# Gate products of a GRU graph network as 2x2 block products with seven multiplications

## The chip, the cores and the metric

The kernel runs on one core of a Trainium2 chip. The metric is the device time of one execution in microseconds (us). The profile is one execution recorded by the hardware profiler. Its engines are PE (TensorE matmuls), PEld (TensorE weight loads, which run beside PE), DVE (VectorE), ACT (ScalarE), POOL (GpSimd) and SP (SyncE, which here only issues transfers).

## The reference

There are 128 graphs of 128 nodes with 256 features, all float32. Layer 0 is a gated graph network of three steps, and layer 1 is a graph attention layer:

```python
A = (adj != 0)
h = relu(layernorm(x))
for i in range(3):
    m = einsum('bnd,de->bne', h, weight[i])
    aggr = einsum('bst,bsd->btd', A, m)
    gi = aggr @ w_ih.T + b_ih ; gh = h @ w_hh.T + b_hh      # 3 gates of 256 each
    r = sigmoid(i_r + h_r) ; z = sigmoid(i_z + h_z)
    n = tanh(i_n + r * h_n)
    h = (1 - z) * n + z * h
x = x + h

h = relu(layernorm(x)); Wh = h @ W; s = Wh.sum(-1)
e = leaky_relu(s[:, :, None] + s[:, None, :], 0.2), -inf where adj == 0
x = x + softmax(e) @ Wh
```

## The kernel before, in words

A group is four graphs (`G`), so 512 nodes (`GN`); there are 32 groups. Features lie on partitions in two chunks of 128 (`KD`) whenever a gate product reads them: `hT` (the state) and `aT` (the aggregate of the state over the graph) are tiles of 128 x 2 x 512. In the setup the kernel transposes `w_hh` into `w_hhT`, and multiplies each layer's message weight with `w_ih` into `w_x`, so that the gates read the aggregate directly.

A GRU step (one layer of one group) is `aggregate` (L191, one 128x128 matmul for each graph and chunk) and two calls of `gru_half`, one for each output chunk `j`. A half forms four sums in PSUM with `gate_sum` (L203): the reset gate r from state and aggregate, the state part and the aggregate part of the candidate n, and the update gate z. Each sum is built of matmuls of 128x128 weights with 512 columns; a half has 12 of them, a step 24. ScalarE evaluates r (L212), n (L219) and z (L222); VectorE forms u (L215, L217) and the new state `new` (L224 to L226). Between layers `T_to_rows` (L181) transposes the state back to node rows, which ScalarE copies (L250), because the aggregation needs them as the stationary operand. VectorE copies the aggregate out of PSUM (L193).

Around the three steps a group has a layer norm with transposes (`normed`, `rows_to_T`, L159), and after them the residual and the second layer norm (L254, L149), the product with `W` (L170), the attention scores (L268 to L282), the transposes of the weights `e` (L286), their product with `Wh` (L294) and the output (L297, L300).

`group` is a generator that yields between these pieces. Two streams of groups (even and odd) are advanced in turns, one seven pieces ahead of the other (`LAG`), so that one stream's other work stands between the GRU steps of the other:

```python
LAG = 7
streams = [stream(0), stream(1)]
for _ in range(LAG):
    next(streams[0])
while streams:
    for s in list(streams):
        if next(s, s) is s:
            streams.remove(s)
```

The three steps of a group follow each other on TensorE, and then come the three steps of the other stream's group. The order within each engine's queue is fixed when the program is built, by a scheduler that takes the program's order as priority and moves ready work forward; the engines then wait for each other through semaphores. PSUM has eight banks of 512 float32 columns: five for the gates (`ps_gate`) and three for everything else (`ps_misc`).

Of the kernel before, what the change touches and what calls it, by code (L numbers as in the profile page):

```python
# [8 lines left out]
F32 = mybir.dt.float32  # L9
I32 = mybir.dt.int32  # L10
AF = mybir.ActivationFunctionType
OP = mybir.AluOpType
AX = mybir.AxisListType

P = 128
G = 4
EPS = 1e-5
ALPHA = 0.2
BIG = 3.0e38
# [3 lines left out]
def kernel(  # L23
# [19 lines left out]
    nc = tc.nc  # L43
    B, N, D = x.shape
    L = weight.shape[0]
    KD = D // P
    NG = B // G
    GN = G * N
    assert N == P and D == 2 * P and B % G == 0

    const = ctx.enter_context(tc.tile_pool(name="const", bufs=1))
    loads = ctx.enter_context(tc.tile_pool(name="loads", bufs=4))
    small = ctx.enter_context(tc.tile_pool(name="small", bufs=4))
    setup_ctx = ExitStack()
    setup = setup_ctx.enter_context(tc.tile_pool(name="setup", bufs=1))
    ps_gate = ctx.enter_context(tc.tile_pool(name="ps_gate", bufs=5, space=bass.MemoryType.PSUM))
    ps_misc = ctx.enter_context(tc.tile_pool(name="ps_misc", bufs=3, space=bass.MemoryType.PSUM))

    loaded = {}

    def load(g):
        if g >= NG:
            return
        xt = loads.tile([P, G, D], F32, name="xt")
        nc.sync.dma_start(xt, x[g * G:(g + 1) * G].rearrange("b n d -> n b d"))
        at = loads.tile([P, G, N], I32, name="at")
        nc.sync.dma_start(at, adj[g * G:(g + 1) * G].rearrange("b n m -> n b m"))
        loaded[g] = xt, at

# [27 lines left out]

    w_t = []
    for name, nat in zip(("w_hhT", "w_ihT"), w_nat):
        t = (const if name == "w_hhT" else setup).tile([P, KD, 3 * D], F32, name=name)  # L100
        for k in range(KD):
            for c0 in range(0, 3 * KD, 3):
                ps = ps_misc.tile([P, 512], F32, name="misc")
                for c in range(3):
                    nc.tensor.transpose(ps[:, c * P:(c + 1) * P],
                                        nat[:, c0 + c, k * P:(k + 1) * P], ident)
                nc.vector.tensor_copy(t[:, k, c0 * P:(c0 + 3) * P], ps[:, :3 * P])
        w_t.append(t)
# [6 lines left out]
    for layer in range(L):  # L115
        wT = setup.tile([P, KD, D], F32, name="w_msgT", bufs=L)
        for e in range(KD):
            ps = ps_misc.tile([P, 512], F32, name="misc")
            for k in range(KD):
                nc.tensor.transpose(ps[:, k * P:(k + 1) * P],  # L120
                                    w_msg[:, layer, k, e * P:(e + 1) * P], ident)
            nc.scalar.copy(wT[:, e, :], ps[:, :D])
        t = const.tile([P, KD, 3 * D], F32, name="w_x", bufs=L)
        for k in range(KD):
            for g0, gn in ((0, 512), (512, 3 * D - 512)):
                ps = ps_misc.tile([P, 512], F32, name="misc")
                for e in range(KD):
                    nc.tensor.matmul(ps[:, :gn], wT[:, e, k * P:(k + 1) * P],  # L128
                                     w_ihT[:, e, g0:g0 + gn], start=(e == 0), stop=(e == KD - 1))
                nc.vector.tensor_copy(t[:, k, g0:g0 + gn], ps[:, :gn])  # L130
        w_x.append(t)

    setup_ctx.close()
    work = ctx.enter_context(tc.tile_pool(name="work", bufs=3))


    def normed(src, name):
        st = small.tile([P, G, 6], F32, name="bn_st")
        mv = small.tile([P, G, 2], F32, name="bn_mv")
        for b in range(G):  # L140
            nc.vector.bn_stats(st[:, b, :], src[:, b, :])  # L141
        for b in range(G):
            nc.vector.bn_aggr(mv[:, b, :], st[:, b, :])
        rs = small.tile([P, G], F32, name="rstd")
        nc.gpsimd.tensor_tensor(rs, mv[:, :, 1], eps, OP.add)
        nc.gpsimd.tensor_tensor(rs, rs, neghalf, OP.pow)  # L146
        y = work.tile([P, G, D], F32, name=name)
        for b in range(G):
            nc.vector.tensor_scalar(y[:, b, :], src[:, b, :], mv[:, b, 0:1], rs[:, b:b + 1],  # L149
                                    op0=OP.subtract, op1=OP.mult)  # L150
        return y
# [33 lines left out]
    def aggregate(m, a):  # L185

        aT = work.tile([P, KD, GN], F32, name="aT")
        for k in range(KD):
            ps = ps_misc.tile([P, 512], F32, name="misc")
            for b in range(G):  # L190
                nc.tensor.matmul(ps[:, b * N:(b + 1) * N], m[:, b, k * P:(k + 1) * P], a[:, b, :],  # L191
                                 start=True, stop=True)
            nc.vector.tensor_copy(aT[:, k, :], ps[:, :GN])  # L193
        return aT

    def gate_sum(c, terms):

        ps = ps_gate.tile([P, GN], F32, name="gate")
        n = len(terms) * KD
        for i in range(n):  # L200
            w, t = terms[i // KD]
            k = i % KD
            nc.tensor.matmul(ps, w[:, k, c * P:(c + 1) * P], t[:, k, :],  # L203
                             start=(i == 0), stop=(i == n - 1))
        return ps

    def gru_half(j, w_ihT, hT, aT, new):

        cr, cz, cn = j, KD + j, 2 * KD + j
        p_r = gate_sum(cr, [(w_hhT, hT), (w_ihT, aT)])  # L210
        r = work.tile([P, GN], F32, name="r")
        nc.scalar.activation(r, p_r, AF.Sigmoid, bias=bias_s[:, cr:cr + 1])  # L212
        p_hn = gate_sum(cn, [(w_hhT, hT)])
        u = work.tile([P, GN], F32, name="u")
        nc.vector.scalar_tensor_tensor(u, p_hn, bias_h[:, cn:cn + 1], r, op0=OP.add, op1=OP.mult)  # L215
        p_in = gate_sum(cn, [(w_ihT, aT)])
        nc.vector.tensor_tensor(u, u, p_in, OP.add)  # L217
        n = work.tile([P, GN], F32, name="n")
        nc.scalar.activation(n, u, AF.Tanh, bias=bias_i[:, cn:cn + 1])  # L219
        p_z = gate_sum(cz, [(w_hhT, hT), (w_ihT, aT)])  # L220
        z = work.tile([P, GN], F32, name="z")
        nc.scalar.activation(z, p_z, AF.Sigmoid, bias=bias_s[:, cz:cz + 1])  # L222
        d = work.tile([P, GN], F32, name="d")
        nc.vector.tensor_tensor(d, hT[:, j, :], n, OP.subtract)  # L224
        nc.vector.tensor_tensor(d, d, z, OP.mult)  # L225
        nc.vector.tensor_tensor(new[:, j, :], n, d, OP.add)  # L226

    def group(g):

        xt, at = loaded.pop(g)  # L230
        load(g + 2)
        a = work.tile([P, G, N], F32, name="a")
        nc.vector.tensor_scalar(a, at, 0.0, None, op0=OP.not_equal)
        y = normed(xt, "h")
        rows = work.tile([P, G, D], F32, name="rows")
        nc.scalar.activation(rows, y, AF.Relu)
        yield
        hT = rows_to_T(rows, "hT", 4)
        yield
        for layer in range(L):  # L240
            aT = aggregate(rows, a)
            new = work.tile([P, KD, GN], F32, name="hT", bufs=4)
            gru_half(0, w_x[layer], hT, aT, new)
            yield
            gru_half(1, w_x[layer], hT, aT, new)
            hT = new
            yield
            if layer < L - 1:
                rows = work.tile([P, G, D], F32, name="rows")
                T_to_rows(hT, lambda b0, ps: nc.scalar.copy(rows[:, b0:b0 + 2, :], ps))  # L250
                yield

        x1 = work.tile([P, G, D], F32, name="x1")
        T_to_rows(hT, lambda b0, ps: nc.vector.tensor_tensor(  # L254
            x1[:, b0:b0 + 2, :], xt[:, b0:b0 + 2, :], ps, OP.add))
        h = normed(x1, "h")
        yield
        h1T = rows_to_T(h, "h1T", 2, AF.Relu)
        yield
        wh = rows_product(h1T, w1, "wh")  # L260
        s = small.tile([P, G], F32, name="s")
# [5 lines left out]
        for b in range(G):  # L267
            nc.tensor.transpose(p_s[:, b, :], s[:, b:b + 1].to_broadcast([P, P]), ident)  # L268
        e = work.tile([P, G, N], F32, name="e")
        nc.vector.tensor_scalar(e, at, 0.0, -BIG, op0=OP.is_equal, op1=OP.mult)  # L270
        nc.vector.tensor_tensor(e, e, p_s, OP.add)
        nc.vector.tensor_tensor(e, e, s[:, :, None].to_broadcast([P, G, N]), OP.add)
        nc.vector.scalar_tensor_tensor(e, e, ALPHA, e, op0=OP.mult, op1=OP.max)
# [13 lines left out]
        eT = work.tile([P, G, N], F32, name="eT")  # L287
        nc.scalar.copy(eT, p_e)
        yield
        o = work.tile([P, G, D], F32, name="o")  # L290
        for b0 in range(0, G, 2):
            ps = ps_misc.tile([P, 2, D], F32, name="misc")
            for b in range(2):
                nc.tensor.matmul(ps[:, b, :], eT[:, b0 + b, :], wh[:, b0 + b, :],  # L294
                                 start=True, stop=True)
            for b in range(2):
                nc.vector.scalar_tensor_tensor(o[:, b0 + b, :], ps[:, b, :],  # L297
                                               rden[:, b0 + b:b0 + b + 1], x1[:, b0 + b, :],
                                               op0=OP.mult, op1=OP.add)
        nc.gpsimd.dma_start(out[g * G:(g + 1) * G].rearrange("b n d -> n b d"), o)  # L300
        yield


# [41 lines left out]
```

## Time and profile before

| | |
|---|---|
| median of 3 runs | 2614.0 us (2613.59 to 2614.19) |
| profiled execution | 2614.36 us, span 2612.6 us, TensorE clock granted 0.994 |
| PE | 2547.0 us busy, 97% of the span |
| PEld | 1357.0 us, 52% |
| DVE | 1282.0 us, 49% |
| ACT | 720.8 us, 28% |
| POOL | 104.1 us, 4% |
| HBM | 27.79 MB read, 16.78 MB written, 17 GB/s over the span |

The span runs from the first to the last instruction. A line of the groups names the program line, engine and operation, what is written and read, the shape and the count, then the busy time and mean duration of one, then the engine's idle time before it and what ended that. Each float32 matmul stands in the trace as two records. Matmuls are pipelined and their ends are modelled, so the distance from start to start tells what one costs in a row of them. In a timeline the columns are the start, the duration and then the group, with the idle time before it and its releaser in brackets.

### The profile page before, as it was taken

Reading aid. Unit: us, or ns where it says so; the run is one execution under the profiler, and the core shown is the slowest. Engines: PE = TensorE matmul, PEld = TensorE weight load, DVE = VectorE, ACT = ScalarE, POOL = GpSimd, SP = SyncE. Lnnn points to the kernel's source line nnn. Section 1 sums busy time; section 2 is a strip of 40 time slices with the busy share of each in tenths; the row PEclk is TensorE's granted clock in tenths of the full one; section 3 lists DMA queues with packets and bytes.
Section 4 is the critical chain, followed back from the end, with each engine's and each line's share of the span. In section 5 each row is a group of like instructions: output and inputs, shape, how many; then the busy total and the mean of one; then the engine's idle time right before and its main releaser. Section 6 shows DMA issues by size and latency. Waiting matters only on the chain.

```text
span 2612.6 us, 22325 instructions
## 1 busy us (share of the span) xinstructions
PE 2547.0 (97%) x8532; PEld 1357.0 (52%) x8532; DVE 1282.0 (49%) x2487; ACT 720.8 (28%) x1063; POOL 104.1 (4%) x166
## 2 busy tenths in 40 slices
PE   6999999999999999999999999999999999999996
PEld 4455555555555555555555555555555555555553
DVE  3355454555545455454554545555454554545544
ACT  1223222332222322222232223322223222222322
POOL 0000000000000000000000000000000000000000
PEclk9999999999999999999999999999999999999998
DMA  3000000000000000000000000000000000000000
GB/s 101 1 21 21 9 21 20 15 18 12 17 21 21 13 21 13 16 21 13 20 21 9 21 21 15 19 13 17 21 21 12 21 9 16 17 9 8 9 1 17
DMA packets 42700, 46.01 MB, mean 18 GB/s; under 512 B 3168, under 2 KB 38496, under 8 KB 42592
## 3 DMA queue, kind: packets, MB, share of 16 engines
q1 hardware_dynamic: 33792, 25.17, 3.2%
q0 software_dynamic: 4608, 16.78, 1.8%
q10 hardware_dynamic: 4192, 2.63, 0.4%
q8 instruction: 67, 1.10, 0.2%
q14 instruction: 41, 0.34, 0.0%
HBM read 27.79 MB, written 16.78 MB: 17 GB/s over the span
## 4 chain that ended last, share of the span: by engine, by line
PE 87%; DVE 6%; issue 2%; ACT 2%; POOL 1%; DMA 1%; ACTq 0%; POOLq 0%; DVEq 0%
PE gate L203 69%; PE misc L191 7%; PE misc L170 4%; PE misc L181 3%; PE misc L294 2%; DVE h L149 1%; DVE bn_st L141 1%; POOL rstd L146 1%; PE misc L159 1%; ACT z L222 1%; DVE hT L226 1%; DVE d L225 1%; ACT L222 1%; PE misc L268 1%; PE misc L128 0%
## 5 line engine op out<-in xcount | busy, mean ns | idle before, releaser
L203 PE MATMUL gate<-hT,w_hhT 128*128 128x512 f32 x2304 | 1096.5, 593 | 0.0
L203 PE MATMUL gate<-aT,w_x 128*128 128x512 f32 x2304 | 1093.5, 596 | 0.0
L203 PEld LDWEIGHTS gate<-aT,w_x 128*128 128x128 f32 x2304 | 427.4, 190 | 553.7 <-issue 477.5
L203 PEld LDWEIGHTS gate<-hT,w_hhT 128*128 128x128 f32 x2304 | 419.2, 191 | 431.3 <-issue 407.2
L215 DVE SCALAR_TENSOR_TENSOR u<-gate,bias_h,r 128x512 f32<-128x512 f32 x192 | 144.0, 750 | 417.7 <-PE gate L203 417.7
L212 ACT ACTIVATE r<-gate,bias_s 128x512 f32<-128x512 f32 x192 | 132.1, 688 | 726.0 <-PE gate L203 726.0
L219 ACT ACTIVATE n<-u,bias_i 128x512 f32<-128x512 f32 x192 | 138.8, 723 | 610.8 <-DVE u L217 540.8
L225 DVE TENSOR_TENSOR d<-d,z 128x512 f32<-128x512 f32 x192 | 132.6, 691 | 238.1 <-ACT z L222 236.5
L222 ACT ACTIVATE z<-gate,bias_s 128x512 f32<-128x512 f32 x192 | 131.8, 687 | 272.4 <-PE gate L203 271.0
L191 PEld LDWEIGHTS misc<-a,rows 128*128 128x128 f32 x1536 | 185.4, 193 | 17.4 <-issue 11.6
L224 DVE TENSOR_TENSOR d<-hT,n 128x512 f32<-128x512 f32 x192 | 131.9, 687 | 124.0 <-ACT n L219 123.9
L191 PE MATMUL misc<-a,rows 128*128 128x128 f32 x1536 | 188.4, 276 | 0.0
L217 DVE TENSOR_TENSOR u<-u,gate 128x512 f32<-128x512 f32 x192 | 131.3, 684 | 116.2 <-PE gate L203 115.8
L193 DVE COPY aT<-misc 128x512 f32<-128x512 f32 x192 | 130.0, 684 | 40.0 <-PE misc L191 39.7
L181 PE MATMUL misc<-ident,hT 128*128 128x128 f32 x768 | 119.9, 278 | 22.1 <-DVE hT L226 16.9
L226 DVE TENSOR_TENSOR hT<-n,d 128x512 f32<-128x512 f32 x192 | 132.3, 689 | 4.4
L181 PEld LDWEIGHTS misc<-ident,hT 128*128 128x128 f32 x768 | 87.6, 141 | 75.4 <-DVE hT L226 48.3
L170 PE MATMUL misc<-w,h1T 128*128 128x256 f32 x512 | 121.6, 386 | 0.6 <-ACT h1T L160 0.5
L170 PEld LDWEIGHTS misc<-w,h1T 128*128 128x128 f32 x512 | 95.7, 192 | 24.8 <-issue 7.2
L250 ACT COPY rows<-misc 128x512 f32<-128x512 f32 x128 | 69.1, 591 | 100.7 <-PE misc L181 100.7
L262 DVE TENSOR_REDUCE s<-wh 128x4 f32<-128x1024 f32 x32 | 39.0, 1220 | 109.3 <-ACT wh L172 109.3
L300 POOL DMA_DIRECT2D out_dram<-o x32 | 25.6, 802 | 1296.7 <-DVE o L297 1259.5
(60 smaller groups left out, 1201.1 us busy)
## 6 DMA issues: line engine op xcount, KB each, us to landing
xt<-in_x_dram SPq DMA_DIRECT2D x32, 512.0 KB, 3.9
out_dram<-o POOLq DMA_DIRECT2D x32, 512.0 KB, 3.4
at<-in_adj_dram SPq DMA_DIRECT2D x32, 256.0 KB, 2.8
w_msg<-in_L_gnn_weight_dram ACTq DMA_DIRECT2D x1, 768.0 KB, 7.0
w_hh_nat<-in_L_gnn_w_hh_dram ACTq DMA_DIRECT2D x1, 768.0 KB, 10.6
w_ih_nat<-in_L_gnn_w_ih_dram ACTq DMA_DIRECT2D x1, 768.0 KB, 13.8
w<-in_L_gnn_W_dram ACTq DMA_DIRECT2D x1, 256.0 KB, 9.0
bias_i<-in_L_gnn_b_ih_dram ACTq DMA_DIRECT2D x1, 3.0 KB, 11.8
```

What stands on the lines that cost most here:

```text
L170: nc.tensor.matmul(ps[:, b, :], srcT[:, k, (b0 + b) * N:(b0 + b + 1) * N], w[:, k, :], start=(k == 0), stop=(k == KD - 1))
L181: nc.tensor.transpose(ps[:, b, k * P:(k + 1) * P], srcT[:, k, (b0 + b) * N:(b0 + b + 1) * N], ident)
L191: nc.tensor.matmul(ps[:, b * N:(b + 1) * N], m[:, b, k * P:(k + 1) * P], a[:, b, :], start=True, stop=True)
L203: nc.tensor.matmul(ps, w[:, k, c * P:(c + 1) * P], t[:, k, :], start=(i == 0), stop=(i == n - 1))
L212: nc.scalar.activation(r, p_r, AF.Sigmoid, bias=bias_s[:, cr:cr + 1])
L215: nc.vector.scalar_tensor_tensor(u, p_hn, bias_h[:, cn:cn + 1], r, op0=OP.add, op1=OP.mult)
L217: nc.vector.tensor_tensor(u, u, p_in, OP.add)
L219: nc.scalar.activation(n, u, AF.Tanh, bias=bias_i[:, cn:cn + 1])
L222: nc.scalar.activation(z, p_z, AF.Sigmoid, bias=bias_s[:, cz:cz + 1])
L224: nc.vector.tensor_tensor(d, hT[:, j, :], n, OP.subtract)
L225: nc.vector.tensor_tensor(d, d, z, OP.mult)
L226: nc.vector.tensor_tensor(new[:, j, :], n, d, OP.add)
```

## The change

The columns of a step's nodes are split into two halves of 256 (`H`), and the feature chunks are the other split, so that each gate's product is a 2x2 block product: two output chunks and two input chunks of the weights, two input chunks and two node halves of the state. It is formed with seven multiplications (Strassen's scheme in Winograd's form) instead of eight, each on 128x128 weights and 256 columns. Sums of weight blocks are formed once in the setup (`block_sums`). Sums of state blocks (`hs`, on GpSimd) and of aggregate blocks (`gs`, on VectorE) are formed in every step (`node_sums`). Partial sums that two outputs share are copied by ScalarE from one PSUM bank to another, where further matmuls add to them; others are copied to SBUF (`t2`, `t3`, `t5`) and added there (`c12` on VectorE, `c22` on GpSimd).

The PSUM banks are now two for x, two for q, two for y (each of the kinds rz and n, one buffer each) and two for `ps_misc`. The copies of the aggregate move from VectorE to ScalarE. The attention reads its mask from `a` instead of `at`, and the output is formed in place in `x1`. The buffers of most work tiles go from three to two, and `w_hhT` and `w_x` become setup tiles, whose memory is used again by the work tiles. The core of the diff:

```diff
-    ps_gate = ctx.enter_context(tc.tile_pool(name="ps_gate", bufs=5, space=bass.MemoryType.PSUM))
-    ps_misc = ctx.enter_context(tc.tile_pool(name="ps_misc", bufs=3, space=bass.MemoryType.PSUM))
+    ps_x = ctx.enter_context(tc.tile_pool(name="ps_x", bufs=1, space=bass.MemoryType.PSUM))
+    ps_y = ctx.enter_context(tc.tile_pool(name="ps_y", bufs=1, space=bass.MemoryType.PSUM))
+    ps_misc = ctx.enter_context(tc.tile_pool(name="ps_misc", bufs=2, space=bass.MemoryType.PSUM))
...
+    def block_sums(t, name):
+        v = t.rearrange("p k (g j m) -> p k g j m", g=3, j=2)
+        a11, a12, a21, a22 = (v[:, k, :, j, :] for j in range(2) for k in range(2))
+        w = const.tile([P, 7, 3, P], F32, name=name, bufs=1 if name == "s_hh" else L)
+        nc.scalar.copy(w[:, 0], a11)
+        nc.scalar.copy(w[:, 1], a12)
+        nc.scalar.copy(w[:, 3], a22)
+        nc.gpsimd.tensor_tensor(w[:, 4], a21, a22, OP.add)
+        nc.gpsimd.tensor_tensor(w[:, 5], w[:, 4], a11, OP.subtract)
+        nc.gpsimd.tensor_tensor(w[:, 6], a11, a21, OP.subtract)
+        nc.gpsimd.tensor_tensor(w[:, 2], a12, w[:, 5], OP.subtract)
+        return [None] + [[w[:, i, q, :] for q in range(3)] for i in range(7)]
...
+    seeded = [ps_y.tile([P, 2, H], F32, name=name) for name in ("y_rz", "y_n")]
+    for y in seeded:
+        nc.tensor.matmul(y.rearrange("p q n -> p (q n)"), ident, w_hhT[:, 0, :512],
+                         start=True, stop=True)
...
-    work = ctx.enter_context(tc.tile_pool(name="work", bufs=3))
+    work = ctx.enter_context(tc.tile_pool(name="work", bufs=2))
...
-            nc.vector.tensor_copy(aT[:, k, :], ps[:, :GN])
+            nc.scalar.copy(aT[:, k, :], ps[:, :GN])
...
-    def gate_sum(c, terms):
...
-    def gru_half(j, w_ihT, hT, aT, new):
...
+    def node_sums(t, name, eng):
+        v = t.rearrange("p k (n m) -> p (k n) m", n=2)
+        b11, b12, b21, b22 = (v[:, i, :] for i in range(4))
+        w = work.tile([P, 4, H], F32, name=name)
+        eng.tensor_tensor(w[:, 0:2, :], v[:, 1::2, :], v[:, 0:2, :], OP.subtract)
+        eng.tensor_tensor(w[:, 2, :], w[:, 1, :], b11, OP.add)
+        eng.tensor_tensor(w[:, 3, :], b21, w[:, 2, :], OP.subtract)
+        return [None, b11, b21, b22, w[:, 3, :], w[:, 0, :], w[:, 2, :], w[:, 1, :]]
+    R, Z, NN = 0, 1, 2
+    def product(bank, i, parts, first):
+        head = None
+        for term in range(max(len(p) for p in parts)):
+            for half, p in enumerate(parts):
+                if term < len(p):
+                    q, w, t = p[term]
+                    ins = nc.tensor.matmul(bank[:, half, :], w[i][q], t[i],
+                                           start=(first and head is None), stop=False,
+                                           skip_group_check=True)
...
+    def gru(layer, hT, hs, gs, new):
+        w = s_x[layer]
+        kinds = (("rz", ([(R, s_hh, hs), (R, w, gs)], [(Z, s_hh, hs), (Z, w, gs)])),
+                 ("n", ([(NN, s_hh, hs)], [(NN, w, gs)])))
+        x, y, q, t2, t3, t5, c12, c22 = ({} for _ in range(8))
+        for kind, parts in kinds:
+            x[kind] = ps_x.tile([P, 2, H], F32, name="x_" + kind)
+            product(x[kind], 1, parts, True)
+            y[kind] = ps_y.tile([P, 2, H], F32, name="y_" + kind)
+            nc.scalar.copy(y[kind], x[kind])
+        for kind, parts in kinds:
+            q[kind] = ps_x.tile([P, 2, H], F32, name="q_" + kind)
+            product(q[kind], 5, parts, True)
+            t5[kind] = work.tile([P, 2, H], F32, name="t5")
+            nc.vector.tensor_copy(t5[kind], q[kind])
+        for kind, parts in kinds:
+            product(y[kind], 6, parts, False)
+            t2[kind] = work.tile([P, 2, H], F32, name="t2")
+            nc.scalar.copy(t2[kind], y[kind])
+        for kind, parts in kinds:
+            product(x[kind], 2, parts, False)
+        for kind, parts in kinds:
+            product(y[kind], 7, parts, False)
+            t3[kind] = work.tile([P, 2, H], F32, name="t3")
+            nc.scalar.copy(t3[kind], y[kind])
+            c22[kind] = work.tile([P, 2, H], F32, name="c22")
+            nc.gpsimd.tensor_tensor(c22[kind], t3[kind], t5[kind], OP.add)
+        for kind, parts in kinds:
+            product(q[kind], 3, parts, False)
+            c12[kind] = work.tile([P, 2, H], F32, name="c12")
+            nc.vector.tensor_tensor(c12[kind], t2[kind], q[kind], OP.add)
+        for kind, parts in kinds:
+            product(y[kind], 4, parts, False)
+        r = work.tile([P, KD, 2, H], F32, name="r", bufs=1)
...
+        for j, n, src in ((0, 0, x), (0, 1, c12), (1, 1, c22), (1, 0, y)):
+            cr, cz, cn = j, KD + j, 2 * KD + j
+            nc.scalar.activation(r[:, j, n, :], src["rz"][:, 0, :], AF.Sigmoid, ...)
+            nc.vector.scalar_tensor_tensor(u[:, j, n, :], src["n"][:, 0, :], bias_h[:, cn:cn + 1],
+                                           r[:, j, n, :], op0=OP.add, op1=OP.mult)
+            nc.vector.tensor_tensor(u[:, j, n, :], u[:, j, n, :], src["n"][:, 1, :], OP.add)
+            nc.scalar.activation(z[:, j, n, :], src["rz"][:, 1, :], AF.Sigmoid, ...)
+        for j in range(KD):
...
+            nc.scalar.activation(nn, nn, AF.Tanh, bias=bias_i[:, cn:cn + 1])
+            nc.vector.tensor_tensor(d, hT[:, j, :], nn, OP.subtract)
+            nc.vector.tensor_tensor(d, d, zz, OP.mult)
+            nc.vector.tensor_tensor(new[:, j, :], nn, d, OP.add)
...
         for layer in range(L):
+            hs = node_sums(hT, "hs", nc.gpsimd)
             aT = aggregate(rows, a)
+            gs = node_sums(aT, "gs", nc.vector)
+            yield
             new = work.tile([P, KD, GN], F32, name="hT", bufs=4)
-            gru_half(0, w_x[layer], hT, aT, new)
-            yield
-            gru_half(1, w_x[layer], hT, aT, new)
+            gru(layer, hT, hs, gs, new)
```

The group still yields as often as before: the two halves with the yield between them have become the sums with the aggregation, a yield, and the whole step.

## The prediction

> **What bounds the kernel now.** I read the page's busy times first, then its chain, then the costliest groups, then TensorE's timeline around two places where one GRU step hands over to the next.
>
> ```profile
> PE 2547.0 (97%) x8532; PEld 1357.0 (52%) x8532; DVE 1282.0 (49%) x2487; ACT 720.8 (28%) x1063; POOL 104.1 (4%) x166
> PE 87%; DVE 6%; issue 2%; ACT 2%; POOL 1%; DMA 1%; ACTq 0%; POOLq 0%; DVEq 0%
> L203 PE MATMUL gate<-hT,w_hhT 128*128 128x512 f32 x2304 | 1096.5, 593 | 0.0
> L203 PE MATMUL gate<-aT,w_x 128*128 128x512 f32 x2304 | 1093.5, 596 | 0.0
> ```
>
> TensorE is the bound in the busy times and in the chain. The gate products are 4608 records, two for each float32 matmul: 48 records in each of 96 GRU steps. Their mean of 0.59 us is not their price, since they overlap. The price is the distance between starts, in the timeline of TensorE alone:
>
> ```profile
> 1333.46 1.88 PE L203 MATMUL gate<-aT,w_x 128*128 128x512 f32 x4
> 1335.18 3.62 PE L170 MATMUL misc<-w,h1T 128*128 128x256 f32 x16
> 1338.63 1.04 PE L181 MATMUL misc<-ident,hT 128*128 128x128 f32 x8
> 1339.50 1.88 PE L203 MATMUL gate<-hT,w_hhT 128*128 128x512 f32 x4
> 1341.22 0.60 PE L268 MATMUL misc<-ident,s 128*128 128x128 f32 x4
> 1341.66 1.95 PE L191 MATMUL misc<-a,rows 128*128 128x128 f32 x16
> 1343.45 1.02 PE L203 MATMUL gate<-hT,w_hhT 128*128 128x512 f32 x2
> ```
>
> From start to start: 512 columns cost 1.72/4 = 0.429 us, 256 columns 3.45/16 = 0.2156, 128 columns 1.79/16 = 0.112. The second place, on all engines, shows how a GRU step hands over to the next layer:
>
> ```profile
> 1362.84 1.89 PE L294 MATMUL misc<-wh,eT 128*128 128x256 f32 x8
> 1363.10 0.69 ACT L222 ACTIVATE z<-gate,bias_s 128x512 f32<-128x512 f32 x1 [1.99 <-PE gate L203]
> 1363.82 0.69 DVE L225 TENSOR_TENSOR d<-d,z 128x512 f32<-128x512 f32 x1 [1.98 <-ACT z L222]
> 1364.83 0.68 DVE L226 TENSOR_TENSOR hT<-n,d 128x512 f32<-128x512 f32 x1
> 1365.56 1.05 PE L181 MATMUL misc<-ident,hT 128*128 128x128 f32 x7
> 1366.14 1.09 ACT L250 COPY rows<-misc 128x512 f32<-128x512 f32 x2 [2.35 <-PE misc L181]
> 1367.31 1.95 PE L191 MATMUL misc<-a,rows 128*128 128x128 f32 x16
> 1369.15 2.02 PE L203 MATMUL gate<-aT,w_x 128*128 128x512 f32 x4
> ```
>
> After the last gate product (1362.84) the state is ready at 1365.5, the transposes, row copies and aggregation follow, and the next aggregate is used at 1369.15: a chain of 6.3 us. TensorE is not idle in it: the other stream's L294 (1.7 us) and early state products cover it.
>
> **The change part by part: TensorE.** A GRU step goes from 48 records of 512 columns to 7 products x 6 matmuls x 2 = 84 records of 256. 48 x 0.429 = 20.60 us; 84 x 0.2156 = 18.11 us; 2.49 us less, times 96 = **-239 us**. The weight load beside each record is 0.19 us long, but L191 starts a load and a matmul every 0.112 us, so loads overlap each other and 0.2156 leaves room. [...]
>
> **Work added beside TensorE**, per step. DVE: gs 0.69 + 2 x 0.41, two t5 copies 1.37, two c12 sums 1.38, u in eight pieces 4 x (0.48 + 0.41) = 3.6 instead of 2.9, less the aT copies 1.37: from 8.4 to 11.9 us (0.41 and 0.48 from L149 and L297, the 256-column rows). Over 96 steps 1282 becomes about 1625, 67% of a shorter span. ACT: two seeds, two t2, two t3, two aT copies at 0.59, and eight pieces of r and z at about 0.45: from 4.2 to 9.7 us; 721 becomes about 1250. Neither becomes the bound.
>
> POOL gets hs (one 128x512, two 128x256) and two c22 sums. No row shows such a sum on POOL. Nearest: the same sum on DVE, 0.69; POOL's own two-input add of 128x4, 0.196; its one-input select of 128x128, 0.295, which scaled four times and doubled for a second input gives 2.4. Between 0.69 and 2.4 I take 1.2, the select scaled by columns. That is about 5 us per step, 20% of the span. c22 has from about 4 us before the last product ends, so 1.2 is hidden, and 2.4 costs up to 0.3 us per step (29 us). [...]
>
> Three waits inside a step have cover. The seed of y (0.3 hand-over + 0.59) is asked for after the fifth product's 2.6 us. The t2 and t3 copies have the 2.6 us of a product on another bank. Behind a waiting seed on ACT stand the next t2 copies and, from the other stream, row copies; behind hs on POOL, which waits for hT, stand rstd (1.2 us) and c22.
>
> **The hand-over** is where I expect the loss. Now each half ends with 2.1 to 2.7 us (z, d, hT). After, the whole step ends at once. Counting from the end of the seventh product: the (1,0) pieces of u 0.9 us, then two halves of three DVE operations at 0.69 = 4.1, and 0.3 hand-over: 5.3 us until hT is whole. Then transposes and hand-over 0.5, two row copies 1.3, the aggregation's rest and hand-over 1.6, two aT copies 1.2, and gs' first sum 0.7: 10.6 us until the fifth product has its gs, against 6.3. The stream's own TensorE work in that time is L181 0.87, L191 1.78, the first product 2.6 and the state half of the fifth 1.3: 6.5 us. So 4.1 us must come from the other stream.
>
> Each group has two such places (layer 0 to 1, layer 1 to 2); the next step after layer 2 belongs to the other stream. At the first the other stream offers L159, L170 and L268 (0.87 + 3.45 + 0.44); at the second L286 and L294 (0.44 + 1.73), and L159 and L191 of its next group. That is enough in sum, but the misc banks go from three to two. L294's banks are emptied by DVE (0.96 us a bank) behind the 5 us of tail, so transposes can stand about 1.4 us, and L170 must wait for L160's copies (1.0). I take 1.2 us idle at the first place, 2.6 at the second, 0.5 at the third: 4.3 x 32 = 138 us.
>
> What is lost at these places now: two groups take 6 x 20.60 + 31.6 (the other records at their distances) = 155.2 us of TensorE, while the middle of the span, about 2540 us, gives each pair 158.8. So 0.6 us per step, 58 us in all, is lost already; net **+80 us**. With the covers all in place this term is zero.
>
> **Start and end.** The setup memory, which the work tiles reuse, is now released after the last block sums: four POOL sums of 384 columns, about 4 us. The first group, with no other stream, stands about 5 us at its first hand-over; the last pays a longer tail (3) and one bare hand-over (4). **+16**. ACT table loads (2 x 1.28 us a group) and POOL beside DVE: **+10**.
>
> Sum, against the profiled execution (span 2612.6, 2614.4 with what lies around it, 0.4 above the median 2614.0): 2614.0 - 239 + 80 + 16 + 10 = **2481 us**.
>
> **Rivals.** *The hand-over decides (slower).* One mechanism, in one place: the 64 hand-overs inside a stream. If the queue order spends L170, L294, L159 and L191 before the chain needs them, or banks are held, nothing covers the 4.1 us, and the bank wait adds 1.4: 5.5 x 64 = 352. That is 2614 - 239 + 352 - 58 + 26 = 2695. It decides from (239 + 58 - 26)/64 = 4.2 us per hand-over. For it: in the trace L159 and L286 stand between two halves, earlier than their place in the program, so fillers do get spent early; state products now cover only 2.6 us where 24 records of 0.429 stood. Against: now the fillers are in place at nearly every hand-over.
>
> *Everything stays covered.* The net term is zero: 2614 - 239 + 26 = 2401. For it: TensorE has work at every moment in my walk if banks are free; against: two banks.
>
> *It doesn't do what it says.* Loads or second accumulations into a seeded bank could stretch the records from 0.2156. From 0.245 (20.60/84) nothing is left. L170 and L294 both speak against it.
>
> **How the numbers follow.** Forecast case 0.48 (2481, itself 2425 to 2560 for idle of 2.5 to 7 us a group and POOL's bounds); all covered 0.2 (2401); hand-over decides 0.27 (2610 to 2700), stretched records 0.05. Range 2395 to 2660: it leaves out the ends of the outer cases. 0.2% is about what a measurement of this kernel can tell from no change. Faster 0.7, same 0.03, slower 0.27.
>
> **What would show it.** Right: 8064 gate records of 256 columns 0.2156 apart inside a product; DVE near 1600, ACT near 1250, POOL near 600 us busy; TensorE's waits named by L181 on DVE hT and by the gate on aT or gs, 1 to 3 us at two places a group. Wrong: records further apart than 0.22, TensorE waiting on seeds or t2 and t3 inside a step, a POOL sum over 2.4 us, or waits over 4 us at the hand-overs.

## The result, and the profile after

The changed kernel takes 2797.9 us (median of four runs, 2797.2 to 2799.0) where the kernel before takes 2614.1 on the same chip: a ratio of 1.070 with a 95% interval of 1.069 to 1.072. The forecast was 2481 with 2660 as its upper end: wrong in sign and outside its range. The profiled execution has a span of 2797.3 us and a granted TensorE clock of 0.961, where it was 0.994.

The busy times and the chain of the page after:

```profile
PE 2433.7 (87%) x11992; PEld 2075.0 (74%) x11992; DVE 1651.8 (59%) x3351; ACT 1228.7 (44%) x2227; POOL 632.6 (23%) x662
PE 44%; DVE 27%; issue 12%; POOL 10%; ACT 6%; DMA 1%; POOLq 0%; DVEq 0%; SPq 0%; ACTq 0%
```

TensorE has less work and a longer span, and the chain that was 87% TensorE is now 44%. The work that was added is as large as forecast on each engine (DVE 1652 for 1625, ACT 1229 for 1250, POOL 633 for 600); what grew is the time in which TensorE does nothing. TensorE's timeline at a first hand-over (layer 0 to layer 1 of one stream) says where:

```profile
1338.66 1.04 PE L187 MATMUL misc<-ident,rows 128*128 128x128 f32 x8
1343.17 0.66 PE L209 MATMUL misc<-ident,hT 128*128 128x128 f32 x2 [3.48 <-ACT u L305]
1343.62 1.91 PE L245 MATMUL x_rz<-hT,s_hh 128*128 128x256 f32 x4
1345.33 1.06 PE L245 MATMUL x_n<-hT,s_hh 128*128 128x256 f32 x2
1346.18 1.49 PE L209 MATMUL misc<-ident,hT 128*128 128x128 f32 x6
1347.46 1.06 PE L245 MATMUL q_rz<-hs,s_hh 128*128 128x256 f32 x2
1348.32 3.77 PE L198 MATMUL misc<-w,h1T 128*128 128x256 f32 x16
1351.93 2.00 PE L219 MATMUL misc<-a,rows 128*128 128x128 f32 x16
```

Three things are to be seen. After the last gate product only L187 of the other stream runs (0.87 us); then TensorE stands 3.48 us for the state. The 3.45 us of L198, which are L170 of the kernel before and were counted as cover, run only after that: at this place they stand in the fixed queue behind the transposes that wait, and in front of the aggregation L219, which they delay. And the four x_rz records after the stand take 1.71 us from start to start, 0.43 each instead of 0.2156. The windows around it show the granted clock (PEclk, the third column from the end) during the stand, after it, and inside the following step:

```profile
core 0: us, PE busy (x) PEld busy (x) DVE busy (x) ACT busy (x) POOL busy (x), PEclk, DMA share, GB/s
1338.70:1343.20 4.50, 1.02 (x10) 0.82 (x8) 3.50 (x7) 3.36 (x7) 0.00 (x0) 0.84 0.00 0
1343.20:1346.20 3.00, 3.00 (x9) 2.35 (x10) 2.08 (x3) 0.00 (x0) 0.70 (x1) 0.50 0.00 0
1356.00:1366.00 10.00, 10.00 (x48) 8.81 (x47) 6.84 (x14) 6.36 (x10) 0.57 (x1) 1.00 0.07 23
```

Why the state is late is on VectorE, whose timeline at the same place follows (its last product's end on TensorE is 1338.66):

```profile
1336.42 0.48 DVE L296 SCALAR_TENSOR_TENSOR u<-c,bias_h,r 128x256 f32<-128x256 f32 x1 [3.51 <-POOL c L281]
...
1337.29 0.68 DVE L285 TENSOR_TENSOR c<-t,q_rz 128x512 f32<-128x512 f32 x1
...
1340.41 0.69 DVE L307 TENSOR_TENSOR d<-hT,u 128x512 f32<-128x512 f32 x1 [0.79 <-ACT u L305]
...
1342.34 0.69 DVE L309 TENSOR_TENSOR hT<-u,d 128x512 f32<-128x512 f32 x1
...
1344.67 0.69 DVE L309 TENSOR_TENSOR hT<-u,d 128x512 f32<-128x512 f32 x1
```

VectorE stands 3.51 us for GpSimd's c22. The piece of u that uses it is queued ahead of c12 (L285), whose inputs are ready earlier, so both halves of the gate tail start late. The state is whole at 1345.4, 6.7 us after the last product. The waits view gives the sum over the span (total, times, longest):

```profile
DVE u L296 <- POOL c L281: 347.5, 96, 3.9
PE misc L209 <- DVE hT L309: 142.2, 93, 3.9
PE misc L209 <- ACT u L305: 70.5, 36, 3.5
```

**The whole difference, from the records.** For every TensorE record between 60 us after the start and 80 us before the end, the distance to the next start was split into its price at full clock (0.429, 0.2156 or 0.111 us), the surplus of records that ran at the halved clock (0.50 granted), and standing. This split is worked out from the trace; its last two columns hold to about 6 us, by how records at the edge of a slow stretch are counted (by the granted clock alone, e9, e14 and e4 have no slow stretch in this part of the span). For the runs on which the argument rests (us):

| run | median us | ratio (95%) | clock | price | standing | slow clock |
|---|---|---|---|---|---|---|
| before | 2614 | | 0.994 | 2421 | 55 | 0 |
| after | 2798 | 1.070 (1.069–1.072) | 0.961 | 2196 | 385 | 80 |
| e1_stale | 2640 | 1.010 (1.009–1.012) | 0.969 | 2189 | 251 | 61 |
| e2_lag2 | 2949 | 1.128 (1.127–1.130) | 0.924 | 2193 | 502 | 116 |
| e3_c22dve | 2699 | 1.033 (1.031–1.034) | 0.965 | 2191 | 296 | 73 |
| e11_hs_dve | 2650 | 1.014 (1.012–1.016) | 0.973 | 2192 | 265 | 54 |
| e13_pieces_only | 2705 | 1.035 (1.033–1.036) | 0.962 | 2195 | 298 | 75 |
| e9_pieces | 2536 | 0.970 (0.969–0.971) | 0.994 | 2191 | 202 | 5 |
| e12_pieces_rev_hs | 2532 | 0.969 (0.967–0.970) | 0.985 | 2190 | 177 | 27 |
| e14_stale_pieces | 2458 | 0.941 (0.939–0.942) | 0.993 | 2185 | 131 | 3 |
| e4_before_misc2 | 2640 | 1.010 (1.008–1.012) | 0.995 | 2424 | 76 | 2 |

From before to after: -225 price + 330 standing + 80 slow clock = +185, against a measured difference of 184. Between the end of the fifth product and the end of the seventh, all 96 steps together stand 1.9 us: nothing is lost inside a step. All of it is lost at the hand-overs: a group's three places together stand 12.4 us and lose 2.5 more to the clock, where 4.3 was forecast. The first place (layer 0 to 1) stands 3.4 us in one stream and 4.6 in the other, the second 5.4 and 4.5, the third (behind layer 2) 1.5 and 5.3, as means over the span.

### The profile page after: what moved, and what is told of

It is laid out like the page before. It is cut to its first block, busy times and chain, and to the rows that moved or that the text cites. A ratio compares the mean times of both kernels' runs of the same rounds, so it can differ in the third digit from the quotient of the medians.

```text
span 2797.3 us, 31817 instructions
## 1 busy us (share of the span) xinstructions
PE 2433.7 (87%) x11992; PEld 2075.0 (74%) x11992; DVE 1651.8 (59%) x3351; ACT 1228.7 (44%) x2227; POOL 632.6 (23%) x662
## 4 chain that ended last, share of the span: by engine, by line
PE 44%; DVE 27%; issue 12%; POOL 10%; ACT 6%; DMA 1%; POOLq 0%; DVEq 0%; SPq 0%; ACTq 0%
PE q_rz L245 8%; PE y_rz L245 7%; PE x_rz L245 6%; POOL c L281 6%; DVE u L296 4%; PE misc L219 4%; DVE d L308 3%; DVE u L298 3%; PE x_n L245 3%; PE y_n L245 3%; ACT u L305 3%; PE misc L198 3%; PE q_n L245 3%; DVE c L285 3%; DVE rows L177 3%
## 5 line engine op out<-in xcount | busy, mean ns | idle before, releaser
L281 POOL TENSOR_TENSOR c<-t,t 128x512 f32<-128x512 f32 x192 | 239.3, 1266 | 847.3 <-ACT t L279 586.9
L245 PE MATMUL y_rz<-hs,s_hh 128*128 128x256 f32 x1152 | 298.1, 379 | 0.0
L245 PE MATMUL y_rz<-gs,s_x 128*128 128x256 f32 x1152 | 295.6, 379 | 0.0
L245 PE MATMUL x_rz<-hT,s_hh 128*128 128x256 f32 x768 | 221.5, 411 | 55.0 <-DVE hT L309 32.0
L245 PEld LDWEIGHTS y_rz<-gs,s_x 128*128 128x128 f32 x1152 | 218.9, 190 | 29.8
L245 PEld LDWEIGHTS y_rz<-hs,s_hh 128*128 128x128 f32 x1152 | 217.7, 190 | 29.0
L219 PEld LDWEIGHTS misc<-a,rows 128*128 128x128 f32 x1536 | 199.8, 204 | 15.6 <-DVE x L338 10.3
L219 PE MATMUL misc<-a,rows 128*128 128x128 f32 x1536 | 203.9, 289 | 6.8 <-DVE x L338 6.8
L245 PEld LDWEIGHTS x_rz<-hT,s_hh 128*128 128x128 f32 x768 | 148.6, 206 | 80.9 <-DVE hT L309 38.0
L245 PE MATMUL x_rz<-aT,s_x 128*128 128x256 f32 x768 | 201.5, 381 | 0.0
L245 PE MATMUL y_n<-hs,s_hh 128*128 128x256 f32 x576 | 171.4, 379 | 0.0
L245 PE MATMUL y_n<-gs,s_x 128*128 128x256 f32 x576 | 171.3, 379 | 0.0
## 6 DMA issues: line engine op xcount, KB each, us to landing
w_hh_nat<-in_L_gnn_w_hh_dram ACTq DMA_DIRECT2D x1, 768.0 KB, 10.6
```

Source lines behind the costliest of these rows:

```text
L245: ins = nc.tensor.matmul(bank[:, half, :], w[i][q], t[i], start=(first and head is None), stop=False, skip_group_check=True)
L281: nc.gpsimd.tensor_tensor(c22[kind], t3[kind], t5[kind], OP.add)
```

## The experiments

Theory A: the loss is at the hand-overs inside a stream, through the dependence of one layer on the one before. Its rivals: B, it is inside the step, in waits for seeds, copies and sums; C, two misc banks are too few. Later texts tell apart whether the fillers are in place but not ready (A2) or transposes that wait hold both misc banks (D); whether the length of the chain (E) or the queue order and the banks (F) set the standing; and whether GpSimd and VectorE are in each other's way (G).

**1. Take the dependence away (e1_stale).** Layers 1 and 2 read the state one layer older, for products, sums and transposes; the amount of work is the same, but the result is no longer that of the reference.

```diff
+        feed = hT
...
-            hs = node_sums(hT, "hs", nc.gpsimd)
+            hs = node_sums(feed, "hs", nc.gpsimd)
...
-            hT = new
+            feed, hT = hT, new
```

> The products, sums and transposes of layers 1 and 2 read the state of one layer earlier, and only the last elementwise update reads the newest state; so the next layer's feed is ready a whole GRU step before it is used, with the same instructions on every engine. Theory A (the hand-over: TensorE stands, and then runs at half clock, while the chain from the last product to the next aggregate runs without cover): 2380 to 2480 us, gate records 0.2156 apart, TensorE's clock back to 0.99. Theory B (waits inside the step: seeds, t2 and t3 copies, c22 on GpSimd in front of c12 in VectorE's queue): stays above 2700. Theory C (two banks for everything else): stays above 2700, since the banks are as scarce as before.

Measured 2639.6: 158 us back, which is below what B and C allow and well above A's 2480. With the 1.9 us above, B falls. 251 us of standing remain. About half of them (128) is at the third place, which the edit leaves as it was: the transposes behind layer 2 still read the newest state there, and the next group's first state is awaited. At the other two no layer depends on the step just before it, and there the waits that the profile names are in part for misc banks, which ScalarE empties before the transposes can write:

```profile
PE misc L209 <- ACT h1T L188: 23.7, 16, 1.5
PE misc L209 <- ACT eT L373: 17.3, 16, 1.1
```

So the late state is not the only thing that leaves TensorE without work.

**2. Let the streams alternate after each part (e2_lag2).** The stagger of the two streams goes from seven parts to two.

```diff
-    LAG = 7
+    LAG = 2
```

> Only the offset of the two streams changes, from 7 pieces to 2, so that the GRU steps of the two groups alternate and a whole step of the other stream (18.1 us of TensorE) stands at each of the 64 hand-overs; the work after the third layer is then bunched. Theory A: 2400 to 2560 us. Theory B and theory C: 2750 to 2850, no better than the changed kernel.

Measured 2949.2, above what any theory gave. Where a whole step of the other stream follows directly, the hand-over is free (first two lines of its TensorE timeline, 0.43 us for two records at full pace). But the attention and output work of both streams now falls together and waits for itself (third line):

```profile
1365.55 0.59 PE L245 MATMUL y_n<-gs,s_x 128*128 128x256 f32 x2
1365.98 1.03 PE L245 MATMUL x_rz<-hT,s_hh 128*128 128x256 f32 x4
...
1311.35 1.11 PE L370 MATMUL misc<-ident,e 128*128 128x128 f32 x4 [5.07 <-DVE e L362]
```

One place in every two groups loses 27 us, 21 of them standing and 6 to the clock. A whole step is cover enough for a hand-over; a stagger that gives it there takes it from the attention.

**3. c22 off GpSimd (e3_c22dve).**

```diff
-            nc.gpsimd.tensor_tensor(c22[kind], t3[kind], t5[kind], OP.add)
+            nc.vector.tensor_tensor(c22[kind], t3[kind], t5[kind], OP.add)
```

> c22 is formed on VectorE (0.69 us each) instead of GpSimd (1.27 us each). Theory A: c22 stands in VectorE's queue ahead of c12 and makes the tail of the step about 1.4 us longer, so 96 x 1.4 = 130 us at most comes back, and VectorE pays some of it: 2660 to 2760. Theory B with c22 as its main wait (3.6 us of VectorE's waiting in each of 96 steps): 2797 - 96 x 3.6 = 2450, at most 2560. Theory C: no change.

Measured 2699.2, inside A's range: 99 us back, though VectorE has 134 us more to do (1785.5 busy). The state is whole 5.7 us after the last product instead of 6.9 (means over the first hand-overs), and standing falls by 89.

**4. One misc bank fewer in the kernel before (e4_before_misc2).**

```diff
-    ps_misc = ctx.enter_context(tc.tile_pool(name="ps_misc", bufs=3, space=bass.MemoryType.PSUM))
+    ps_misc = ctx.enter_context(tc.tile_pool(name="ps_misc", bufs=2, space=bass.MemoryType.PSUM))
```

> The kernel before with two misc banks instead of three, and nothing else. Theory C: 2700 or more. Theory A: within 1.5% of 2614, because the short hand-over of the kernel before keeps its cover.

Measured 2639.7: the third bank was worth 26 us in the kernel before, where C asked for 86 or more. What two banks cost in the changed kernel, whose gates hold six banks where they held five, no run shows.

**5. Other staggers, c22 on VectorE (e5_c22_lag8, e6_c22_lag9, e7_c22_lag5), and the kernel before (e8_before_lag8).** Each is the one line `LAG = 7` changed to 8, 9, 5, and 8.

> c22 on VectorE as in the run before (2699 us), and the streams 8 pieces apart instead of 7. The other stream's normed rows are then transposed before the GRU step and not at its hand-over, so that the product with W has its input when the hand-over comes; the same for each other filler, one piece earlier. Theory A2 (the fillers are in the right place but not ready, because ScalarE and VectorE, which must prepare them, are busy with the step's own tail): 2540 to 2650. Theory D (two misc banks: transposes that have half of their state hold both and keep every filler out, ready or not): 2670 to 2740.

> As the run with 8 pieces, but 9: the product with W now falls before the first step of the other stream, so the first hand-over has only the scores and the second only the output product. Theory A2: readier but less work at the hand-overs, between the run with 8 and 2699, about 2600 to 2690. Theory D: 2670 to 2740.

> c22 on VectorE and 5 pieces: one of a group's two hand-overs between layers has a whole GRU step of the other stream in it, the other has the work before layer 0 or after layer 2. In the run with 2 pieces such a place stood 0.01 us. Theory A2: a third of the standing of 2699 goes, 2580 to 2660. Theory D: 2670 to 2800, because two streams then want the two banks at once.

> Control: the kernel before with 8 pieces instead of 7. Its hand-overs stand some 0.6 us a step, so there is little to win: both theories 2590 to 2640.

Measured 2703.9, 2968.5, 2831.8 and 2613.2 (ratios 1.035, 1.136, 1.084, 1.000). With 8 the same fillers stand at the same places as with 7: the scheduler, not the stagger, had put them there, and the run, though in D's range, could not part D from A2. With 9 TensorE waits above all for the late state, with 5 for it and for the next group's normed rows (first line with 9, the other two with 5), and neither theory had priced that:

```profile
PE misc L209 <- DVE hT L309: 320.4, 101, 4.6
PE misc L187 <- DVE rows L177: 80.5, 32, 4.3
PE misc L187 <- ACT rows L319: 68.0, 16, 6.8
```

These runs say that no stagger tried wins the loss back, and no more.

**6. The gate tail in pieces (e9_pieces, e10_pieces_rev).** On top of e3, tanh and the three state operations run on each 128x256 quarter as soon as its u is there, instead of on whole halves after all four. e10 also transposes the later nodes first.

```diff
-        for j in range(KD):
...
+            nn, cols = u[:, j, n, :], slice(n * H, (n + 1) * H)
...
+            d = work.tile([P, H], F32, name="d", bufs=4)
+            nc.vector.tensor_tensor(d, hT[:, j, cols], nn, OP.subtract)
+            nc.vector.tensor_tensor(d, d, z[:, j, n, :], OP.mult)
+            nc.vector.tensor_tensor(new[:, j, cols], nn, d, OP.add)
```

> c22 on VectorE as in the run with 2699 us, and the last part of a step (tanh and the three VectorE operations) is done for each of the four pieces of 256 columns as soon as its u is there, instead of for each half of 512 at the end. VectorE does 12 operations of about 0.42 us instead of 6 of 0.69. After the last product only the (1,0) piece is left: about 3.3 us until the state is whole, instead of 5.7. Theory E (the length of the chain from the last product to the next aggregate sets the standing): up to 2.4 us at 94 hand-overs, 2480 to 2600. Theory F (the queue order and the two banks set it, so a shorter chain is not used): 2640 to 2720.

> As the run in pieces, and the transposes take the second node half first, whose state is whole about 3 us before the last product ends. Theory E: a further 20 to 60 us below the run in pieces, because half of the transposes and one row copy leave the chain. Theory F: no difference over 20 us.

Measured 2535.8 and 2538.5: e9 is 3.0% faster than before, 262 us faster than after. Its page and its TensorE timeline at a second hand-over:

```profile
PE 2370.6 (94%) x11992; PEld 2008.3 (79%) x11992; DVE 1795.7 (71%) x4119; ACT 1270.0 (50%) x2419; POOL 391.0 (15%) x470
```

```profile
1322.69 1.89 PE L374 MATMUL misc<-wh,eT 128*128 128x256 f32 x8
1324.42 1.03 PE L245 MATMUL x_rz<-hT,s_hh 128*128 128x256 f32 x4
1325.28 0.59 PE L245 MATMUL x_n<-hT,s_hh 128*128 128x256 f32 x2
1326.96 1.13 PE L245 MATMUL q_rz<-hs,s_hh 128*128 128x256 f32 x4 [1.09 <-POOL hs L230]
```

The filler L374 is in the first wait, the state part of the first product follows at once and at full pace, since it needs one quarter of the state, and the longest stand is 1.1 us. The time is in E's range, but not by E's step: the whole state was expected 3.3 us after the last product and comes after 6.2, later than in e3 (5.7). What comes earlier is its first part, 1.0 to 4.2 us before the last product ends instead of 3.2 to 4.0 us after it, so that the first product's state part runs in the wait. The next gs is 1.7 us earlier (11.7 us after the last product for 13.4, means over both streams' first and second places). The queue is in another order too, and no run parts that from the early quarter. Reversing the transposes gains nothing, where E asked for 20 to 60 us.

**7. The state sums off GpSimd (e11_hs_dve, e12_pieces_rev_hs).** On e3 and on e10, `hs = node_sums(hT, "hs", nc.vector)`.

> c22 and hs on VectorE, so that GpSimd has only the norms' small operations and the output transfer. Theory E: the fifth product's state half is ready 0.5 us earlier, and L177, which took 0.9 us instead of 0.41 beside GpSimd's sums, is short again; VectorE has 1.5 us more a step: 2650 to 2700. Theory G (GpSimd and VectorE in each other's way is the main remaining loss): under 2600.

> All three together: c22 and hs on VectorE, the step's end in pieces, the second node half first. Theory E: 2420 to 2560, below the kernel before. Theory F: 2620 to 2720.

Measured 2649.8 and 2531.8: 49 us on e3, 7 on e10. e11 is at the lower bound of E's range and e12 in it; G, which asked for under 2600, falls, and F's ranges are missed in e9 and e12. The sum itself is shorter on VectorE (in the kernel after its first 128x512 part took 1.28 us on GpSimd, the same part of gs 0.69 on VectorE), and L177 no longer runs beside it: the same line on xt has a median of 884 ns in e3 and 408 in e11. In the kernel after it looks so at a second hand-over, while GpSimd sums:

```profile
1376.87 3.29 DVE L177 TENSOR_SCALAR rows<-xt,bn_mv,rstd 128x256 f32<-128x256 f32 x4
```

e12 is the fastest version in which every layer reads the state of the layer before it: 0.969 (0.967 to 0.970) of the time before, 4 us faster than e9.

**8. Each half alone, and the rest (e13_pieces_only, e14_stale_pieces).** Still open was why c22 and the pieces give 262 us together when c22 alone gives 99. e13 is e9 with c22 back on GpSimd. e14 is e9 with the older state of e1, and like it gives another result.

> The changed kernel with its last part in pieces of 256, c22 left on GpSimd. If the two edits act on different parts of the chain, this is 2797 - 162 = 2635 or a little less. If c22's place in VectorE's queue is what holds the chain, pieces alone bring little: 2720 to 2790. If pieces alone do it all, because the first state products then cover the wait: 2540 to 2580.

> c22 on VectorE, the last part in pieces, and the feed of layers 1 and 2 one layer older as in the first run. This is the price of everything that is left when neither c22 nor the dependence between layers makes TensorE wait. If the hand-overs between layers are all that is left: 2400 to 2440. If the standing comes from ScalarE's and VectorE's queues and the banks, which serve both streams in a fixed order whatever the dependence: 2470 to 2530.

e13 measured 2704.9, which none of its three cases gave: the pieces alone give 93, so 70 us appear only with both. The split of the records shows them: standing adds up (-87 and -89 alone, -183 together), but the slow clock is 73 and 75 with either alone and 5 with both. In e3 stands of 3.5 us remain, in e13 of 2.2, in e9 none over 1.1. e13 also shows a drop without 3 us of standing in one piece; its windows around a stand of 2.18 us (1413.5 to 1415.7) read 1.00 and then 0.68:

```profile
1413.00:1415.00 2.00, 0.53 (x3) 0.12 (x1) 2.00 (x7) 0.00 (x0) 0.61 (x1) 1.00 0.00 0
1415.00:1417.00 2.00, 1.29 (x3) 1.12 (x4) 2.00 (x6) 0.51 (x1) 1.38 (x2) 0.68 0.00 0
```

e14 measured 2458.0, between what the two theories gave it. Without the dependence between layers the seven products bring 156 us in this kernel; 131 us of standing stay even then. Its waits name, above all, the transposes behind layer 2, which still read the newest state, and the next group's L187:

```profile
PE misc L209 <- DVE hT L306: 49.4, 64, 2.6
PE misc L187 <- DVE rows L177: 17.0, 16, 3.7
```

## Why the prediction was wrong

**What held.** The records inside a product are 0.2156 apart, so the price fell as forecast: -225 us in the middle, of -239 over all steps. The rival of stretched records falls: inside a step the trace shows no stretch. GpSimd's 128x512 sum took 1.27 us for 1.2, VectorE, ScalarE and GpSimd are about as busy as the sum said, the start is 5.0 us later for 4, and the waits inside a step are covered.

**What failed is the hand-over term**: +80 net in the sum, +330 of standing and +80 of slow clock in the trace. Four steps of it were wrong.

*The chain was priced 10.6 us to the fifth product's gs and is 14.8 at the first place, 13.9 at the second.* These are means over both streams. Two of its parts are off. The whole state was to come after 5.3 us and comes after 6.9. The prediction took VectorE to be free for the tail when the seventh product ends; it counted c22's 1.27 us as hidden, with a wait on no one, though the piece of u that needs it stands ahead of c12 in VectorE's queue. At the place shown c12 had its q_rz at 1335.4 and ran at 1337.29, after that piece. That is the cost the prediction's own question should have found: what is queued behind the instruction that waits. e3 prices it at 99 us. The aggregation's products were to end 8.7 us after the last product (5.3 + 0.5 + 1.3 + 1.6) and end after 13.3 at the first place: 14.3 in the stream where L198 stands in front of them, 12.4 in the other.

*Cover was counted as a sum.* L187, L198 and L352 are 4.8 us together and the chain lacked 4.1, so the place seemed covered but for 1.2. But here a filler covered a wait only where its input was ready then and where it stood ahead of the waiting instruction in TensorE's queue. At the place shown L198 met neither: its h1T copies were on ScalarE behind r, z and tanh, at 1341.0, and it stood behind the transposes. What ran in the first wait was 0.87 us of L187, at the second place 0.44 of L370. That is one stream. In the other both fillers stand where they were counted, straight behind the last product (its first place, then its second):

```profile
1258.34 3.62 PE L198 MATMUL misc<-w,h1T 128*128 128x256 f32 x16
1262.42 0.30 PE L209 MATMUL misc<-ident,hT 128*128 128x128 f32 x1 [0.47 <-DVE hT L309]
1286.98 1.89 PE L377 MATMUL misc<-wh,eT 128*128 128x256 f32 x8
1290.98 1.13 PE L245 MATMUL x_rz<-hT,s_hh 128*128 128x256 f32 x4 [2.11 <-DVE hT L309]
```

These two places together stand 8.7 us and lose 1.5 to the clock; in the stream where the fillers come late it is 9.1 and 2.2. So the order of the fillers explains little of the loss. The main step that failed is the length of the chain, 14.0 and 13.6 us to gs even where the fillers were in place: at that first place 14.0 less the stream's own 6.5 and the fillers' 3.9 is 3.6, and 3.4 were measured.

*The third place was taken at 0.5 us.* It stands 5.3 us in one of the two streams and 1.5 in the other. There TensorE waits for the state as at the other places, and for the next group's first state and normed rows:

```profile
PE x_rz L245 <- ACT hT L188: 23.0, 15, 1.5
PE misc L187 <- DVE rows L177: 15.2, 16, 4.3
```

*A stand was priced at its length.* After a stand of 3.48 us the granted clock was 0.50 over the next three microseconds, and such stretches came to 80 us. The half clock did not wait for the end of the stand: it began 2.1 us into it, and in e13 it came with a stand of 2.18 us (last section).

The rival "the hand-over decides" had two of the three places and the sign, with 2695 us. Its 5.5 us for each of 64 hand-overs is close to the measured 5.4 (4.5 of standing and 0.9 to the clock), in part by luck: it left a chain of 10.6 us uncovered, where a longer chain was partly covered. What it lacks is the third place, which it left out.

**What stays open.** Of the 131 us of standing in e14 only the waits above are named. Why the scheduler put L198 and L377 behind the transposes in one stream and ahead of them in the other was not tried: no run fixed the order by hand. Nor did any run give the changed kernel a third misc bank, so what waiting for banks costs in it stays open.

## What to carry to other kernels

When a change cuts the bound engine's work, price the dependent chain between its stages first: what used to end in two halves and now ends at once makes a wait out of work that was hidden. Price it with what stands in each engine's queue ahead of its links, c22 here. Cover is not a sum of microseconds: ask of each filler whether its input is ready in the wait and whether it stands ahead of the waiting instruction in the queue. On TensorE price standing above its length where the trace shows a lower clock behind it: away from the ends of the span each drop to 0.50 in the kernel after followed 3.41 us with at least 1.79 us of standing, and in e12 one followed three short stands. Several small repairs can then be worth more together than apart (here 262 us, and 99 and 93).

## What was not expected of the hardware

The clock also fell without one long gap. In every trace here that has it away from the ends of the span, the half clock (0.50) began on a grid of 3.41 us, lasted 3.41 us or a multiple of it, and followed a grid interval of which TensorE stood a good part: in the kernel after 30 stretches of 3.41 us and 12 of 6.83 (from 60 us after the start to 80 us before the end), behind intervals with 1.79 to 3.37 us of standing. The changed kernel (first two lines) worked 1.30 us in the interval before the drop. e12 (last two) has no stand over 1.1 us, but three of 0.7 to 0.8 close together, and worked 1.74 (columns as in the windows above):

```profile
1338.39:1341.80 3.41, 1.30 (x10) 0.96 (x9) 2.48 (x6) 2.67 (x7) 0.00 (x0) 1.00 0.00 0
1341.80:1345.21 3.41, 2.04 (x6) 1.80 (x7) 3.15 (x6) 1.00 (x2) 0.00 (x0) 0.50 0.00 0
1324.19:1327.60 3.41, 1.74 (x9) 1.08 (x10) 3.41 (x11) 1.17 (x2) 0.80 (x1) 1.00 0.05 17
1327.61:1331.02 3.41, 3.41 (x18) 3.41 (x17) 1.45 (x4) 1.64 (x2) 0.00 (x0) 0.50 0.39 136
```

As worked out from the traces of all runs, each interval at full clock with more than 2.03 us of standing was followed by the half clock and none with less than 1.47 was; in between both occur (in the kernel after, 1.79 with a drop and 1.99 without). So the longest stand alone does not tell: with none over 2.2 us e13 lost 75 us, and of two kernels with none over 1.1, e12 lost 27 and e9 next to nothing.

VectorE's float32 128x256 tensor_scalar from SBUF (L177) took 0.41 us with none of GpSimd's two-input sums beside it and 0.88 where they ran beside it for nine tenths of its time or more (medians of 132 and 47 in the kernel after). With the state sums and c22 on VectorE (e11) the median on xt is 0.41. Why L177 takes longer beside them no run shows. L354, another tensor_scalar from SBUF, took 0.42 us for twice as many columns (median in the kernel after); none of those sums ran beside it.
